# The last 16 tokens of a spectral convolution: one matrix per lag in place of a fourth 8-token block

## The chip, the cores and the metric

The kernel runs on one core of a Trainium2 chip. The metric is the device time of one execution in microseconds (us), the median over the runs shown. The core has a matrix engine (TensorE, PE in the profile; its weight loads are listed apart as PEld), a vector engine (VectorE, DVE), an activation engine (ScalarE, ACT), GpSimd (POOL), and a queue that here issues nearly all transfers (SyncE, SP).

## The reference, cut to what matters

The whole is a four-layer network on 16 images of 128 channels and 28 x 28 = 784 positions: an L1-distance convolution, two quantized convolutions, an additive-attention block with a mixture of experts, and a linear-attention block with a spectral filter (STU). All is fp32. The change touches only the last, the spectral filter on the 784 tokens of each image:

```python
U_plus  = irfft(rfft(phi) * rfft(u))[:sl]            # causal convolution of u with 16 filters
U_minus = irfft(rfft(phi) * rfft(u * sgn))[:sl] * sgn    # the same with alternating signs
out = einsum('btkd,k,kde->bte', U_plus, sigma ** 0.25, M_phi_plus)
    + einsum('btkd,k,kde->bte', U_minus, sigma ** 0.25, M_phi_minus)
    + sum_i shift(u, i) @ M_u[i]                     # three shifts
```

It is computed for the first 784, 392, 196 and 98 tokens with four sets of matrices, and mixed with weights that depend on parameters only. So output token t is a sum over lags l of u[t - l] times a 128 x 128 matrix that depends on the lag alone.

## The kernel before, in words

**Layout of the work.** Images go in pairs. Eight "pairs" of the L1 convolution come one after the other; each is a list of *steps* (264 steps in the first two pairs, 208 in the other six). In a step four filters get their absolute-difference tiles `d` from VectorE (max, L1139 and L1141) or ScalarE (abs, L1137), and TensorE sums each over channels with a selector of 32 columns (L1126): four such products run in four strips of the array. The tiles `d` come from a ring of 10 buffers.

**Other layers beside it.** Everything else is written as generators that yield either `EV` (other engines next) or `PE` (TensorE next). They are run in lanes: `convs` (group norm and quantized convolutions), `chain` (the token lane: `head`, `attend`, `experts`, `linear_attention`, `normed`), and `conv_out` (the spectral filter, `spectral(b)`). The attention scores (`scores`, ScalarE tanh at L727 with TensorE sums at L710) run as `units`, two in a step. In each step a lane gets `rate` turns, rounded over time, so with `RATE_Y` = 0.85 the spectral lane takes 0.85 turns a step. What comes in which order on each engine is thus the order in which the program emits it; TensorE's order is fixed to it. A lane that has nothing ready lets its turn pass. `normed(b)` waits until `spectral(b - 1)` is through.

After the last pair there are no more distances. In this *tail* (`stage["alone"]`) the remaining scores, the token lane and the spectral lane go on, with `RATE_Z` = 0.75 spectral turns a step; scores are then made by VectorE adds and one large tanh (L720, L722).

**The spectral filter of one image.** `normed` leaves the normalized tokens by channel in `ut` (two zero columns ahead) and, transposed by 128, the even and the odd tokens in `up` (two parities, four blocks of up to 128 tokens: 128 + 128 + 128 + 8 = 392). `spectral(b)` makes the even outputs (`to` = 0) and then the odd ones (`to` = 1), 392 columns each, in the accumulator `acc`: three products with `mats_ar` (the shifts of the reference, L1004), and 32 *jobs*. A job has one filter and one parity of the filter's taps: a banded matrix `band` [128, 392] is fetched, four products with the four blocks of `up` as weights (of 392, 264, 136 and 8 columns, L1019) give the filtered tokens `u`; ScalarE copies them to `us` (L1029), and in the next turn a product with the job's mixing matrix `mat` adds them to `acc` (L1022). So there are 64 jobs per image and 1024 in all. `fetch(n)` asks for band and mat two jobs ahead, on SP, into three buffers each.

The matrices are made once: `token_constants` builds the 32 bands, `spectral_weights` the 32 mixing matrices `mats` in DRAM (`mats[k]` with the even taps' filter k, `mats[16 + k]` with the odd). Both belong to the token lane's first work, during pair 0. `sc`, the score matrix, is their scratch before the first scores.

Of the kernel before, what the change touches and what calls it, by code (L numbers as in the profile page):

```python
# [16 lines left out]
T = HW * HW  # L17
# [48 lines left out]
TW = NT * P  # L66
HB = 98

WIN = T // 2 + 2
SPAN = T // 2 + TB  # L70
TH = T // 2
# [6 lines left out]
RING, ROWS = 10, 14  # L78


RATE_X, RATE_Y, RATE_S, RATE_C, RATE_A, RATE_0, RATE_T, RATE_Z = 1.2, 0.85, 2.0, 1.0, 1.5, 0.7, 2.0, 0.75


EV, PE = "other engines", "TensorE"
# [86 lines left out]
def kernel(ctx: ExitStack, tc: tile.TileContext, a: dict, out: bass.AP):  # L171
# [282 lines left out]


    band = [scratch.tile([P, TH], F32, name=f"band{i}") for i in range(2 * NK)]
    mats = [scratch.tile([P, P], F32, name=f"mat{i}") for i in range(2 * NK)]
    mats_ar = [scratch.tile([P, P], F32, name=f"mat_ar{j}") for j in range(NAR)]

    eb_rows = scratch.tile([P, NT, P], F32, name="eb_rows")  # L460
# [58 lines left out]
    def spectral_weights():  # L519


        yield EV
        lw = two.tile([P, NS], F32, tag="lw", name="lw")
        nc.sync.dma_start(lw, rows_of(a["L3_ffn_log_weights"], P))
        gu = two.tile([P, NS], F32, tag="gu", name="gu")
        nc.sync.dma_start(gu, rows_of(a["L3_ffn_gumbel"], P))
        sg = const.tile([P, NK], F32, name="sg")
        nc.sync.dma_start(sg, rows_of(a["L3_ffn_sigma"], P))
        quarter = const.tile([P, NK], F32, name="quarter")
        nc.vector.memset(quarter, 0.25)  # L530
        nc.gpsimd.tensor_tensor(sg, sg, quarter, ALU.pow)
        yield EV
        nc.vector.tensor_tensor(lw, lw, gu, ALU.add)
        s1 = two.tile([P, 1], F32, tag="s1", name="s1")
        nc.vector.tensor_reduce(s1, lw, AX.X, ALU.max)
        nc.vector.tensor_scalar(lw, lw, s1, None, ALU.subtract)
        nc.scalar.activation(lw, lw, AF.Exp)
        yield EV
        nc.vector.tensor_reduce(s1, lw, AX.X, ALU.add)
        nc.vector.reciprocal(s1, s1)  # L540
        soft = const.tile([P, NS], F32, name="soft")
        nc.vector.tensor_scalar(soft, lw, s1, None, ALU.mult)
        hard = const.tile([P, NS], F32, name="hard")
        nc.vector.tensor_reduce(s1, soft, AX.X, ALU.max)
        nc.vector.tensor_scalar(hard, soft, s1, None, ALU.is_equal)
        nc.vector.tensor_tensor(hard, hard, falling[:, :NS], ALU.mult)
        nc.vector.tensor_reduce(s1, hard, AX.X, ALU.max)
        nc.vector.tensor_scalar(hard, hard, s1, None, ALU.is_equal)
        w = const.tile([P, NS], F32, name="mix")
        nc.vector.tensor_tensor(w, hard, soft, ALU.subtract)  # L550
        nc.vector.tensor_tensor(w, w, soft, ALU.add)

        nc.vector.tensor_scalar(mask, ones[:, :1].to_broadcast([P, TH]), hard[:, 0:1], None, ALU.mult)
        for i in range(1, NS):
            nc.vector.tensor_scalar(mask[:, : TH >> i], mask[:, : TH >> i], hard[:, i : i + 1], None, ALU.add)
        yield EV

        def mixed(dst, src):
            nc.vector.tensor_scalar(dst, src[:, 0], w[:, 0:1], None, ALU.mult)
            for i in range(1, NS):  # L560
                nc.vector.scalar_tensor_tensor(dst, src[:, i], w[:, i : i + 1], dst, ALU.mult, ALU.add)

        sources = [a["L3_ffn_M_u"][:, j] for j in range(NAR)]
        sources += [a["L3_ffn_M_phi_" + name][:, k] for k in range(NK) for name in ("plus", "minus")]
        loaded = []

        def fetch():
            if sources:
                t = spare(NS * P).rearrange("p (s e) -> p s e", s=NS)
                nc.sync.dma_start(t, sources.pop(0).rearrange("s d e -> d s e"))  # L570
                loaded.append(t)

        for _ in range(3):
            fetch()
        yield EV
        for j in range(NAR):
            yield EV
            m = three.tile([P, P], F32, tag="mat", name=f"m_ar{j}")
            mixed(m, loaded.pop(0))
            fetch()  # L580
            nc.sync.dma_start(mats_ar[j], m)
        for k in range(NK):
            yield EV
            me = three.tile([P, P], F32, tag="mat", name=f"m_even{k}")
            mo = three.tile([P, P], F32, tag="mat", name=f"m_odd{k}")
            plus = loaded.pop(0)
            mixed(me, plus)
            mixed(mo, loaded.pop(0))
            dif = plus[:, 0]
            nc.vector.tensor_tensor(dif, me, mo, ALU.subtract)  # L590
            nc.vector.tensor_tensor(me, me, mo, ALU.add)
            nc.vector.tensor_scalar(me, me, sg[:, k : k + 1], None, ALU.mult)
            nc.vector.tensor_scalar(mo, dif, sg[:, k : k + 1], None, ALU.mult)
            fetch()
            fetch()
            nc.sync.dma_start(mats[k], me)
            nc.sync.dma_start(mats[NK + k], mo)
        nc.gpsimd.memset(sc, 1.0)
        yield EV

# [351 lines left out]
    def normed(b):  # L952

        yield EV
        t = state.pop(b)[0]
        n4 = one.tile([P, NT, P], F32, tag="ln", name=f"n4_{b}")
        yield from layer_norm(n4, t, 1e-5, f"s{b}")
        while b and b - 1 not in spectral_out:
            yield EV
        yield from to_channels(lambda lo, n: in_rows(ut[:, 2 + lo : 2 + lo + n]), n4, f"n4{b}")  # L960
        tt = one.tile([P, T], F32, tag="tt", name=f"tt{b}")
        yield from to_channels(lambda lo, n: in_rows(tt[:, lo : lo + n]), t, f"t3{b}")
        up = one.tile([P, 2, 4, P], F32, tag="up", name=f"up{b}")
        for par in range(2):
            yield PE
            q = ps(f"up{b}")
            for i in range(4):
                s = 2 + par + 2 * P * i
                nc.tensor.transpose(blk(q, i), ut[:, s : s + 2 * P - 1 : 2], ident)
            yield EV  # L970
            nc.scalar.copy(up[:, par], q.rearrange("p (n c) -> p n c", c=P))
        spectral_in[b] = tt, up

    def spectral(b):
# [19 lines left out]
        for to in range(2):  # L994
            acc = psout.tile([P, 512], F32, tag="acc", name=f"out{b}_{to}")
            for j in range(NAR):
                m = two.tile([P, P], F32, tag="mar", name=f"mar{b}_{to}_{j}")
                nc.sync.dma_start(m, mats_ar[j])
                mar[j] = m
                if j == 0:  # L1000
                    yield EV
                yield PE
                s = 2 + to - j
                nc.tensor.matmul(acc[:, :TH], m, ut[:, s : s + 2 * TH - 1 : 2], start=j == 0, stop=False)  # L1004
            mine = range(32 * to, 32 * to + 32)
            if to == 0:
                fetch(0)
                fetch(1)
            copied = []
            for n in [*mine, None]:  # L1010
                yield PE
                if n is not None:
                    _, k, odd = jobs[n]
                    fetch(n + 2)
                    t, m = got.pop(n)
                    q = small(f"u{b}_{n}")
                    for i in range(4):
                        w = TH - P * i
                        nc.tensor.matmul(q[:, P * i : TH], up[:, to ^ odd, i, :], t[:, :w], start=i == 0, stop=i == 3)  # L1019
                while len(copied) > (stage["alone"] and n is not None):  # L1020
                    u, m0, lag = copied.pop(0)
                    nc.tensor.matmul(acc[:, lag:TH], m0, u[:, : TH - lag], start=False, stop=n is None and not copied)  # L1022
                if n is not None:
                    yield EV
                    if stage["alone"]:
                        u = rows_pool.tile([P, WIN], F32, tag="row", name=f"us{b}_{n}")
                    else:
                        u = two.tile([P, TH], F32, tag="u", name=f"us{b}_{n}")
                    nc.scalar.copy(u[:, :TH], q[:, :TH])  # L1029
                    copied.append((u, m, odd and (to ^ odd)))  # L1030
            yield EV
            s = tt[:, to : to + 2 * TH - 1 : 2]
            y = two.tile([P, TH], F32, tag="y", name=f"ys{b}_{to}")
            nc.vector.tensor_tensor(y, acc[:, :TH], mask, ALU.mult)
            nc.vector.tensor_tensor(s, s, y, ALU.add)
        nc.sync.dma_start(out[b], tt)
        spectral_out.add(b)

# [176 lines left out]
```

## Time and profile before

| | |
|---|---|
| median of three runs | 12013.93 us (12013.17 to 12015.77) |
| the profiled execution's own time | 12013.72 us |
| its span in the profile | 12012.0 us |
| pair 0 / pair 1 / pairs 2 to 7 end at | 916 / 2155 / 3506, 4876, 6252, 7622, 9003, 10393 us |
| tail | 10393 to 12012 us |
| spectral images that end before the tail | 11 of 16 (the 11th at 10349 us) |

How to read it: "busy" is the time in which an engine executes something; an engine's busy share says nothing on what it waits for. TensorE instructions are pipelined, so the durations shown for them overlap and the distance of their starts says more. A stretch is a part of the span between two times, for which busy time is given by engine. A line such as L1019 is a line of the kernel; "u<-band,up" says that a tile u is made of tiles band and up.

### The profile page before, as it was taken

Reading aid. Unit: us, or ns where it says so; the run is one execution under the profiler, and the core shown is the slowest. Engines: PE = TensorE matmul, PEld = TensorE weight load, DVE = VectorE, ACT = ScalarE, POOL = GpSimd, SP = SyncE. Lnnn points to the kernel's source line nnn. Section 1 sums busy time; section 2 is a strip of 40 time slices with the busy share of each in tenths; the row PEclk is TensorE's granted clock in tenths of the full one; section 3 lists DMA queues with packets and bytes.
Section 4 is the critical chain, followed back from the end, with each engine's and each line's share of the span. In section 5 each row is a group of like instructions: output and inputs, shape, how many; then the busy total and the mean of one; then the engine's idle time right before and its main releaser. Section 6 shows DMA issues by size and latency. Waiting matters only on the chain. (4 is left out here: it accounts for less than half of the span.)

```text
span 12012.0 us, 240466 instructions
## 1 busy us (share of the span) xinstructions
PE 11409.5 (95%) x99948; PEld 5214.0 (43%) x99948; DVE 10731.9 (89%) x15051; ACT 10263.3 (85%) x14568; POOL 186.2 (2%) x144
## 2 busy tenths in 40 slices
PE   8989999999999999999999999999999999999999
PEld 3333333444444444444444444444444444454446
DVE  9898789899999999899999999999999889988882
ACT  8884998979979899797998979889898898988882
POOL 0000000000000000000000000000000000000000
PEclk9999999999999999999999999999999999999999
DMA  0110000010110101001010110101110111011113
GB/s 24 58 32 5 1 1 6 17 34 27 33 32 18 35 28 32 24 28 33 26 38 17 31 33 25 31 26 31 34 31 19 29 31 34 27 54 51 54 54 97
DMA packets 376034, 372.49 MB, mean 31 GB/s; under 512 B 40296, under 2 KB 362144, under 8 KB 374944
## 3 DMA queue, kind: packets, MB, share of 16 engines
q1 hardware_dynamic: 374512, 355.35, 10.4%
q8 instruction: 787, 12.89, 0.4%
q14 instruction: 303, 2.48, 0.1%
q10 hardware_dynamic: 432, 1.77, 0.0%
HBM read 340.19 MB, written 16.78 MB: 30 GB/s over the span
## 5 line engine op out<-in xcount | busy, mean ns | idle before, releaser
L727 ACT ACTIVATE row<-wi 128x394 f32<-128x394 f32 x9904 | 5297.0, 625 | 254.1 <-PE sp L710 251.8
L1126 PE MATMUL acc<-d,sel_m 128*32 128x392 f32 x38656 | 5217.3, 502 | 144.2 <-DVE d L1141 133.3
L1139 DVE TENSOR_SCALAR d<-pad,w 128x1568 f32<-128x1568 f32 x4832 | 4783.5, 1031 | 456.9 <-PE acc L1126 454.3
L1126 PE MATMUL acc<-d,sel_a 128*32 128x392 f32 x18176 | 4502.8, 500 | 71.1 <-ACT d L1137 68.8
L1137 ACT ACTIVATE d<-pad,w 128x1568 f32<-128x1568 f32 x2272 | 3581.7, 1609 | 597.7 <-PE acc L1126 581.0
L1141 DVE SCALAR_TENSOR_TENSOR d<-pad,w,d 128x1568 f32<-128x1568 f32 x2112 | 3863.1, 1846 | 8.7
L1126 PEld LDWEIGHTS acc<-d,sel_m 128*32 128x32 f32 x38656 | 1714.0, 111 | 2121.2 <-issue 1653.9
L710 PE MATMUL sp<-row,vz 128*32 128x394 f32 x19808 | 2086.9, 495 | 1.1 <-ACT row L727 1.1
L1126 PEld LDWEIGHTS acc<-d,sel_a 128*32 128x32 f32 x18176 | 1349.4, 110 | 1111.1 <-issue 857.7
L1019 PE MATMUL u<-band,up 128*128 128x392 f32 (+3 forms) x8192 | 1752.9, 355 | 16.4 <-ACT us L1029 14.0
L1019 PEld LDWEIGHTS u<-band,up 128*128 128x128 f32 x8192 | 1330.0, 190 | 964.6 <-issue 281.2
L710 PEld LDWEIGHTS sp<-row,vz 128*32 128x32 f32 x19808 | 728.1, 110 | 1052.9 <-issue 791.1
L722 ACT ACTIVATE th<-th 128x1576 f32<-128x1576 f32 x660 | 969.8, 1521 | 118.4 <-DVE th L720 109.7
L720 DVE TENSOR_SCALAR th<-wi 128x394 f32<-128x394 f32 x2640 | 923.3, 420 | 12.0 <-PE sp L710 9.2
L1022 PE MATMUL out<-us,mat 128*128 128x392 f32 (+1 forms) x2048 | 923.6, 534 | 0.0
L1029 ACT COPY us<-u 128x392 f32<-128x392 f32 x1024 | 491.4, 480 | 480.6 <-PE u L1019 478.5
L710 PE MATMUL sp<-th,vz 128*32 128x394 f32 x5280 | 514.1, 503 | 47.7 <-ACT th L722 47.5
L884 DVE SCALAR_TENSOR_TENSOR t<-ex,gate,t 128x128 f32<-128x128 f32 x896 | 310.7, 347 | 83.9 <-PE ex L880 75.7
L1022 PEld LDWEIGHTS out<-us,mat 128*128 128x128 f32 x2048 | 311.7, 192 | 21.3 <-issue 8.3
L710 PEld LDWEIGHTS sp<-th,vz 128*32 128x32 f32 x5280 | 136.8, 109 | 340.7 <-issue 168.0
L880 PE MATMUL ex<-ew,xt 128*128 128x512 f32 x448 | 236.0, 609 | 37.1 <-DVE t L884 33.2
L795 PE MATMUL av<-vx,sc 128*128 128x129 f32 x1568 | 202.4, 282 | 37.3 <-DVE sc L784 18.7
(257 smaller groups left out, 4415.9 us busy)
## 6 DMA issues: line engine op xcount, KB each, us to landing
band<-band SPq DMA_DIRECT2D x1024, 196.0 KB, 2.4
mat<-mat SPq DMA_DIRECT2D x1024, 64.0 KB, 2.0
L_conv_w<-q_L_conv_w SPq DMA_DIRECT2D x16, 576.0 KB
ew<-in_L_ffn_expert_w_dram SPq DMA_DIRECT2D x16, 512.0 KB
eb<-eb_rows SPq DMA_DIRECT2D x16, 448.0 KB, 4.2
x<-in_x_dram SPq DMA_DIRECT2D x8, 784.0 KB
band<-band_out SPq DMA_DIRECT2D x32, 196.0 KB, 1.9
xr<-in_x_dram SPq DMA_DIRECT2D x8, 784.0 KB, 4.1
```

Of the source, the lines that this page charges most:

```text
L710: nc.tensor.matmul(sp[32 * j : 32 * j + 32, lo : lo + WIN], vz[:, 32 - m : 64 - m], rows[j], start=False, stop=m == Q - 1, skip_group_chec ...
L720: nc.vector.tensor_scalar(th[:, j, :], wi[:, i + Q * j : i + Q * j + WIN], wi[:, i + Q * j : i + Q * j + 1], None, ALU.add)
L722: nc.scalar.activation(th, th, AF.Tanh)
L727: nc.scalar.activation(rows[j], wi[:, i + Q * j : i + Q * j + WIN], AF.Tanh, bias=wi[:, i + Q * j : i + Q * j + 1])
L884: nc.vector.scalar_tensor_tensor(t[:, i, :], q[:, e * P : (e + 1) * P], gate[:, g : g + 1], t[:, i, :], ALU.mult, ALU.add)
L1019: nc.tensor.matmul(q[:, P * i : TH], up[:, to ^ odd, i, :], t[:, :w], start=i == 0, stop=i == 3)
L1022: nc.tensor.matmul(acc[:, lag:TH], m0, u[:, : TH - lag], start=False, stop=n is None and not copied)
L1029: nc.scalar.copy(u[:, :TH], q[:, :TH])
L1126: nc.tensor.matmul(accs[c][32 * j : 32 * j + 32, :NCK], sel[kind][:, 31 - m : 63 - m], d[:, 14 * c : 14 * c + 14, :], start=False, stop=n ...
L1137: nc.scalar.activation(d, window(pad, k, 0, 2 * HW), AF.Abs, bias=w0[:, k, f : f + 1], scale=-1.0)
L1139: nc.vector.tensor_scalar(d, window(pad, k, 0, 2 * HW), w0[:, k, f : f + 1], None, ALU.max)
L1141: nc.vector.scalar_tensor_tensor(d, window(pad, k, 0, 2 * HW), w0[:, k, f : f + 1], d, ALU.max, ALU.add)
```

## The change

The 16 last tokens of an image (784 - 6 x 128, `LAST`) no longer take part as a fourth block of 8 tokens per parity. `up` keeps three blocks per parity, and a job has three products. What is left out is the contribution of the last 16 input tokens to the last 16 output tokens. It is made anew, by lag: for each of the lags 0 to 15 one matrix [128, 128], which is the sum over all filters of the filter's tap at that lag times its mixing matrix. These 16 matrices are made once, at the end of `spectral_weights`, by products of `lag_w` (the taps, 32 filters x lags) with the mixing matrices, read back flat from DRAM, and stored in DRAM as `lag_mats`.

In `spectral`, the first accumulator gets 16 more columns (392 to 407), in which the first `mats_ar` product starts the sum with 408 columns (the last 16 of them over zeros); six turns follow with the lag matrices in groups of three (the last with one), fetched two groups ahead into the buffers of `band`: lag l multiplies the first 16 - l of the last 16 tokens into columns 392 + l to 407. The first two jobs' `fetch` calls move into these turns. At the end of the even half these 16 columns are added to the last 16 tokens of the result by one more VectorE operation. `RATE_Y` goes from 0.85 to 0.93.

```diff
+LAST = T - 6 * P
...
-RATE_X, RATE_Y, RATE_S, RATE_C, RATE_A, RATE_0, RATE_T, RATE_Z = 1.2, 0.85, 2.0, 1.0, 1.5, 0.7, 2.0, 0.75
+RATE_X, RATE_Y, RATE_S, RATE_C, RATE_A, RATE_0, RATE_T, RATE_Z = 1.2, 0.93, 2.0, 1.0, 1.5, 0.7, 2.0, 0.75
...
-    mats = [scratch.tile([P, P], F32, name=f"mat{i}") for i in range(2 * NK)]
+    mats_all = scratch.tile([2 * NK, P * P], F32, name="mats")
+    mats = [mats_all[i].rearrange("(d e) -> d e", e=P) for i in range(2 * NK)]
+
+    lag_mats = scratch.tile([LAST, P, P], F32, name="lag_mats")
...
             nc.sync.dma_start(mats[k], me)
             nc.sync.dma_start(mats[NK + k], mo)
+
+        phi = a["L3_ffn_phi"]
+        lag_w = const.tile([2 * NK, 32], F32, name="lag_w")
+        nc.gpsimd.memset(lag_w, 0.0)
+        for odd in range(2):
+            nc.sync.dma_start(
+                lag_w[odd * NK : odd * NK + NK, odd : LAST : 2],
+                bass.AP(phi.tensor, odd * NK * phi.shape[1] + HB - 1, [[phi.shape[1], NK], [1, LAST // 2]]))
+        yield EV
+        flat = sc.rearrange("p n c -> p (n c)")
+        rhs = {}
+
+        def fetch_flat(g):
+            if g < 8:
+                rhs[g] = flat[: 2 * NK, 2048 * (g % 2) : 2048 * (g % 2) + 2048]
+                nc.sync.dma_start(rhs[g], mats_all[:, 2048 * g : 2048 * g + 2048])
+
+        fetch_flat(0)
+        fetch_flat(1)
+        for _ in range(4):
+            yield EV
+        for g in range(8):
+            yield PE
+            q = ps(f"lag{g}")
+            for j in range(4):
+                nc.tensor.matmul(q[32 * j : 32 * j + 32, :], lag_w, rhs[g][:, 512 * j : 512 * j + 512],
+                                 start=True, stop=True)
+            yield EV
+            fetch_flat(g + 2)
+            o = flat[:, 4096 + 512 * (g % 4) : 4608 + 512 * (g % 4)]
+            nc.scalar.copy(o, q)
+            for j in range(4):
+                nc.sync.dma_start(lag_mats[:, 16 * g + 4 * j : 16 * g + 4 * j + 4, :],
+                                  o[32 * j : 32 * j + LAST].rearrange("l (d e) -> l d e", e=P))
         nc.gpsimd.memset(sc, 1.0)
...
-        up = one.tile([P, 2, 4, P], F32, tag="up", name=f"up{b}")
+        up = one.tile([P, 2, 3, P], F32, tag="up", name=f"up{b}")
...
-            for i in range(4):
+            for i in range(3):
                 s = 2 + par + 2 * P * i
                 nc.tensor.transpose(blk(q, i), ut[:, s : s + 2 * P - 1 : 2], ident)
             yield EV
-            nc.scalar.copy(up[:, par], q.rearrange("p (n c) -> p n c", c=P))
+            nc.scalar.copy(up[:, par], q[:, : 3 * P].rearrange("p (n c) -> p n c", c=P))
...
-                nc.tensor.matmul(acc[:, :TH], m, ut[:, s : s + 2 * TH - 1 : 2], start=j == 0, stop=False)
+                n = TH + LAST if to == 0 and j == 0 else TH
+                nc.tensor.matmul(acc[:, :n], m, ut[:, s : s + 2 * n - 1 : 2], start=j == 0, stop=False)
             mine = range(32 * to, 32 * to + 32)
             if to == 0:
-                fetch(0)
-                fetch(1)
+
+                lags = {}
+
+                def fetch_lags(l):
+                    if l < LAST:
+                        n = min(3, LAST - l)
+                        lags[l] = three.tile([P, TH], F32, tag="band", name=f"lags{b}_{l}")[:, : n * P].rearrange(
+                            "p (l e) -> p l e", e=P)
+                        nc.sync.dma_start(lags[l], lag_mats[l : l + n].rearrange("l d e -> d l e"))
+
+                fetch_lags(0)
+                fetch_lags(3)
+                for l0 in range(0, LAST, 3):
+                    yield PE
+                    fetch_lags(l0 + 6)
+                    m = lags.pop(l0)
+                    for l in range(l0, min(l0 + 3, LAST)):
+                        s = 2 + T - LAST
+                        nc.tensor.matmul(acc[:, TH + l : TH + LAST], m[:, l - l0, :], ut[:, s : s + LAST - l],
+                                         start=False, stop=False)
+                    if l0 == 9:
+                        fetch(0)
+                    if l0 == 12:
+                        fetch(1)
...
-                    for i in range(4):
+                    for i in range(3):
                         w = TH - P * i
-                        nc.tensor.matmul(q[:, P * i : TH], up[:, to ^ odd, i, :], t[:, :w], start=i == 0, stop=i == 3)
+                        nc.tensor.matmul(q[:, P * i : TH], up[:, to ^ odd, i, :], t[:, :w], start=i == 0, stop=i == 2)
...
             nc.vector.tensor_tensor(s, s, y, ALU.add)
+            if to == 0:
+                s = tt[:, T - LAST : T]
+                nc.vector.scalar_tensor_tensor(s, acc[:, TH : TH + LAST], mask[:, TH - 1 : TH], s, ALU.mult, ALU.add)
```

## The prediction

> **What bounds the kernel now.** I read the page's busy shares first, then the stretches (busy time of each engine between two times), then the timeline inside one job, the groups by shape, and the DMA issues.
>
> ```profile
> PE 11409.5 (95%) x99948; PEld 5214.0 (43%) x99948; DVE 10731.9 (89%) x15051; ACT 10263.3 (85%) x14568; POOL 186.2 (2%) x144
> ...
> DVE d L1139 <- PE acc L1126: 454.3, 375, 5.6
> ```
>
> All three engines are near full, TensorE (PE) most; VectorE (DVE) idles 454 us for TensorE to release a tap buffer. The shares are averages, so I cut the span. The next columns are the stretch, its length, and busy time of PE, weight loads (PEld), DVE, ACT.
>
> ```profile
> 3877.00:3923.00 46.00, 46.00 (x433) 20.47 (x426) 40.26 (x33) 45.61 (x74) 0.00 (x0) 1.00 0.14 36
> 5356.00:5402.00 46.00, 44.25 (x406) 19.82 (x408) 41.41 (x34) 46.00 (x75) 0.00 (x0) 1.00 0.14 36
> 6841.00:6887.00 46.00, 44.74 (x401) 20.25 (x402) 43.03 (x36) 46.00 (x75) 0.00 (x0) 1.00 0.13 36
> ...
> 6904.00:7004.00 100.00, 100.00 (x887) 47.84 (x889) 95.32 (x110) 94.44 (x150) 0.00 (x0) 1.00 0.14 38
> ...
> 5881.00:6010.00 129.00, 111.76 (x1113) 45.54 (x1109) 126.78 (x166) 127.44 (x200) 4.13 (x2) 0.95 0.02 8
> ...
> 10391.00:11680.00 1289.00, 1231.66 (x8719) 612.49 (x8711) 1140.72 (x3597) 1084.86 (x991) 20.93 (x16) 0.99 0.17 49
> 11680.00:12012.00 332.00, 315.06 (x1487) 226.65 (x1483) 81.81 (x263) 71.61 (x147) 4.64 (x4) 0.99 0.35 96
> ```
>
> Four regimes. The first three rows are 40 to 85 us into a spectral image (7 to 14 steps after its first mats_ar product): ScalarE (ACT) is full. Later in an image (fourth row) TensorE is full. Between images (fifth) DVE and ACT are at 98 to 99%, TensorE at 87%. After the last pair (sixth, seventh: the tail) TensorE has 95%, DVE 88% and then 25%. So TensorE time taken from a spectral image pays in the second and fourth regime, not in the first and third.
>
> Next, one job where nothing else runs (last image):
>
> ```profile
> 11940.22 0.64 PEld L1019 LDWEIGHTS u<-band,up 128*128 128x128 f32 x4
> 11940.79 0.30 PEld L1022 LDWEIGHTS out<-us,mat 128*128 128x128 f32 x2
> 11941.23 0.85 PEld L1019 LDWEIGHTS u<-band,up 128*128 128x128 f32 x3
> ...
> L1019 PE MATMUL u<-band,up 128*128 128x8 f32 x2048 | 291.2, 214 | 0.0
> ...
> L1029 ACT COPY us<-u 128x392 f32<-128x392 f32 x1024 | 491.4, 480 | 480.6 <-PE u L1019 478.5
> ```
>
> A matmul is two records here (1024 jobs, 2048 records of each width). Jobs start 2.217 us apart. Starts within a job advance by 0.329 twice (392 columns), 0.222 twice (264), 0.115 twice (136). At 8 columns a record's stream is nothing, but its 128-column weight load is not: the first L1022 load starts at 11940.79, 0.11 after the previous one, the next 0.11 later, and the second L1022 product waits until 11941.23. Counted back by one 0.329 stream, the first L1022 product effectively starts at 11940.898; without the 8s it would start 0.115 after the last 136-column record (11940.558), at 11940.673. **The fourth block costs 0.225 us a job**, two weight loads of 0.112.
>
> **What the Trainium skill says.** "TensorE: Matmul & The Clock Gate", section "LDWEIGHTS (loading the stationary operand)": load time goes with the columns of the weights, about 107 ns for 128, whatever the contraction. The trace agrees (0.110 to 0.116 between such loads; the record's 190 ns is longer). "Perfetto Trace Analysis", section "Identifying the Most-Contended Engine": matmul busy share is a poor measure of distance to the limit; hence I use starts, not the 214 ns of the 8-column row. "TensorE: Matmul & The Clock Gate", section "Why this matters for your kernels": outputs at different groups of 32 PSUM partitions run concurrently; the tap sums agree, four starting some 6 ns apart every 0.33 us. "DMA: Bandwidth & Descriptors", section "Latency and other measured facts": about 2 us fixed cost; the median landings of mat and band, 2.0 and 2.4 us, agree.
>
> **The change part by part.** *Removed:* 64 jobs x 0.225 = 14.4 us of TensorE per image, 230 in all; two of eight transposes per image (0.118 each, 0.2); a quarter of the up copy on ACT (586 ns for 512 columns, some 0.12 us less, 32 times, 4 us in all: nothing beside the rest).
>
> *Added per image:* 16 lag products, two records each, bound by weight loads as the nearest row is (lg, L822, 8 columns: starts 0.111 to 0.112 apart): 32 x 0.112 = 3.6 us. They come in six turns. A turn of full-array matmuls among the four-strip tap sums pays for switching: around 7010.6 us the entry takes 0.42 instead of 0.33, its first record 0.43 instead of 0.33, the exit 0.42: 0.3 us x 6 = 1.8 us (0.6 in the tail, where full-array work is usually next). Sixteen more columns in one product: 0.03. One DVE operation of 16 columns (0.15 to 0.2 by the 128x1 and 128x56 rows): 3 us in all; the next image half's first product waits for it, taken as nothing, 0 to +3. Net TensorE per image: -14.4 - 0.2 + 3.6 + 1.8 = **-9.2 us, -147 over 16**.
>
> *Moved, turns of the lane.* An image takes 75 turns before, 81 after (six lag turns). At RATE_Y 0.85 and 0.93 that is 88 and 87 steps, so the supply of later stages does not move. But TensorE work of a step with jobs stays put: 0.85 x (2.217 + 0.3) = 2.14 before, 0.93 x (1.992 + 0.3) = 2.13 after. The saving does not sit in these steps; there are fewer of them (64/0.85 = 75, 64/0.93 = 69), and 6.5 steps with lag products instead. These fall just where the first three rows show ACT full. What helps there is the missing us copy: 0.85 x 0.48 = 0.41 us a step, 2.6 us an image. One step fewer with spectral work (6.7 to about 6.1 us): 0.6. So **3.2 us of 9.2; 11 images end before the tail: -35 us**. Bounds: 0 (ACT stays full) and -101 (all of it).
>
> *Tail:* 5 images, 14.4 + 0.2 - 3.6 - 0.6 = 10.4 each, 52 us. TensorE is the limit, DVE at 88% takes part of it back: I take 80%, -42; bounds -20 and -52. RATE_Z stays 0.75 a step, so an image takes 108 steps instead of 100, and the token lane's normed(12), which waits for spectral_out(11), comes 8 steps later: the heads and scores behind it start later. Steps without scores are short and the work is done later, so 0, up to +16 steps of 3.9 us, two heads late, +62.
>
> *Fetches:* per image six DMAs of up to 196 KB in 512-byte pieces through the band buffers, on SP. Nothing shows such a size in such pieces; nearest are band (2.4 us) and mat (2.0 us), so 2 to 4 us. They are asked for two turns ahead, 2 x 7 us beside the taps, so hidden. fetch(0) and fetch(1) now wait behind lag groups, hidden by two turns or more there. In the last image turns take 1 us and the bands come late once: +5 (0 to +10).
>
> *Setup in pair 0:* eight turns of four 512-column products. The four strips should run together: 2 x 0.43 (start spacing of ex, 512 columns) + 0.3 = 1.2 us, 9 in all; one after another 30. Eight ACT copies of 0.59, 4.7. Its 42 DMAs at 0.32 us issue take 13 us of SP, beside a token lane that has nothing due until pair 1's levels (mats end at 706 us, head(0)'s wi is at 1144). In that stretch TensorE is at 92%: +8, bounds 0 and +30.
>
> Sum: -35 - 42 + 5 + 8 = **-64 us**. The profiled execution took 12013.72 us for a span of 12012.0; 12013.7 - 64 = 11950. The median of the runs, 12013.93, is the same to 0.2 us.
>
> **Rivals.** *B, TensorE binds everywhere:* the 95% and its release waits speak for it, the rows with ACT full against it. Full 147 less setup and fetch, 13: 11880. *C, the gain stays hidden:* ACT and DVE hold the pairs, and late heads in the tail take half: -21 + 13 = -8, 12006. For: 98 to 99% of DVE and ACT between images; against: TensorE at 100% in the fourth row. *D, slower, lag fetches late:* TensorE takes instructions in order, so a lag product waiting for its matrix holds that step's tap sums, and behind them the release of tap buffers to DVE and ACT. 96 groups x 2.4 us = 230: 12014 - 64 + 230 = 12180. It decides from 64/96 = 0.67 us a group. Against it: two turns of cover, and band fetches at the same distance, which TensorE hardly waits for. *E, not what it says:* were the load of mat, not the 8-column block, the limit before L1022, removing the block would save only 0.03 a job, 30 us, less than the 86 us of lag turns and 13 of setup: 12080. The starts above exclude it nearly.
>
> **Numbers.** A (forecast, 11915 to 11985) 0.50, B 0.17, C 0.22, D 0.07, E 0.04. Within 0.2% (24 us, what a measurement of this kernel can tell from no change) lies most of C, 0.16; faster is A, B and the rest of C, 0.73; slower is D and E, 0.11. The range reaches from B's end to C: 11875 to 12010.
>
> **What would show it.** Right: L1019 with three widths; L1022's first product 0.11 us after the last 136-column record; jobs 1.99 us apart in the last image; steps with lag products a little shorter and ACT-full; pairs 5 to 7 us shorter each; a tail of some 1585 us; lag records 0.11 apart. Wrong: TensorE waits on a lag fetch, heads in the tail later than scores, or lag products slower than 0.112 a record.

## The result, and the profile after

After the change the median of four runs is **11938.65 us** (11936.35 to 11939.38), against 12014.41 for four runs of the kernel before beside it: ratio 0.9936, 95% interval 0.9921 to 0.9951, 75.8 us less. The profiled execution has a span of 11937.4 us, 74.6 less than before. Forecast were 11950 and a gain of 64.

| | before | after | difference | forecast |
|---|---|---|---|---|
| pairs 0 and 1 (setup among them) | 2156.1 us | 2157.1 us | +1.0 | +8 |
| pairs 2 to 7 | 8237.0 | 8170.8 | -66.2 | -35 |
| tail (after the last pair) | 1618.9 | 1609.5 | -9.4 | -37 (-42, and +5 of fetches) |

So the sum was met by three terms that missed: the pairs gained nearly twice what was forecast, the tail a quarter. Most of the experiments below look for the reason of the third row.

From the page after, the shares and, of the list of waits, VectorE's and ScalarE's for tap buffers:

```profile
PE 11327.5 (95%) x98444; PEld 5069.4 (42%) x98444; DVE 10741.9 (90%) x15107; ACT 10251.1 (86%) x14546; POOL 178.7 (1%) x145
...
ACT d L1202 <- PE acc L1191: 496.7, 237, 12.6
DVE d L1204 <- PE acc L1191: 433.0, 346, 6.0
```

TensorE is busy 82 us less and keeps its 95%, since the span fell with it. VectorE's wait was 454.3, ScalarE's 581.0. Now the stretches from 20 to 66 us into a spectral image, in three of the pairs. That is where the lag turns stand after the change; the prediction's first three rows lie 20 us later in their images. First before (columns as in the prediction):

```profile
3857.00:3903.00 46.00, 46.00 (x431) 20.07 (x423) 45.86 (x48) 45.61 (x75) 3.02 (x1) 0.97 0.12 30
5336.00:5382.00 46.00, 43.73 (x396) 19.30 (x391) 42.81 (x41) 46.00 (x77) 1.27 (x1) 1.00 0.13 35
6822.00:6868.00 46.00, 44.40 (x403) 20.22 (x402) 45.93 (x41) 46.00 (x77) 0.00 (x0) 1.00 0.13 35
```

And after, with a stretch later in an image, and the tail up to its last image and in it:

```profile
3880.00:3926.00 46.00, 42.33 (x410) 18.45 (x413) 45.85 (x45) 46.00 (x76) 3.61 (x1) 0.96 0.11 29
5342.00:5388.00 46.00, 44.45 (x425) 18.55 (x421) 43.35 (x38) 46.00 (x74) 0.00 (x0) 1.00 0.11 30
6816.00:6862.00 46.00, 44.98 (x415) 21.00 (x413) 46.00 (x44) 46.00 (x72) 0.00 (x0) 1.00 0.11 29
...
6904.00:7004.00 100.00, 100.00 (x887) 46.22 (x886) 94.25 (x110) 91.61 (x145) 0.00 (x0) 1.00 0.15 41
...
10328.00:11617.00 1289.00, 1214.56 (x8511) 583.10 (x8504) 1169.66 (x3710) 1095.58 (x997) 21.18 (x16) 0.99 0.18 50
11617.00:11938.00 321.00, 302.78 (x1295) 210.32 (x1293) 67.59 (x223) 73.93 (x153) 4.63 (x4) 0.98 0.40 109
```

The regimes are the same: ScalarE full early in an image, TensorE full later. One row stands out: the first 1289 us of the tail hold *more* VectorE work than before (1169.66 against 1140.72 us), though the change adds only one short operation per image there. 17 of these 29 us belong to the scores (VectorE's work on `th` in the same stretches is 935.48 us against 918.88). Work has come into the tail.

One job of the last image, from the timeline of weight loads, and from the groups by shape the narrowest tap block and the largest lag product:

```profile
11811.82 1.62 PEld L1081 LDWEIGHTS u<-band,up 128*128 128x128 f32 x6
11813.37 0.31 PEld L1084 LDWEIGHTS out<-us,mat 128*128 128x128 f32 x2
11813.82 1.62 PEld L1081 LDWEIGHTS u<-band,up 128*128 128x128 f32 x6
...
L1081 PE MATMUL u<-band,up 128*128 128x136 f32 x2048 | 405.6, 280 | 0.0
L1065 PE MATMUL out<-ut,lags 128*128 128x16 f32 x32 | 6.2, 270 | 0.0
```

Six loads and two a job where there were eight and two; the blocks have 392, 264 and 136 columns; jobs follow 1.993 us apart (2.217 before; forecast 1.99). The lag product's 270 ns is, like the 214 ns of the old 8-column row, not a cost: six records of a turn start within 0.579 us, 0.116 apart (forecast 0.112).

### The profile page after: what moved, and what is told of

It reads as the page before. It is cut to its first block, busy times and chain, and to the rows that moved or that the text cites. A ratio compares the mean times of both kernels' runs of the same rounds, so it can differ in the third digit from the quotient of the medians.

```text
span 11937.4 us, 237767 instructions
## 1 busy us (share of the span) xinstructions
PE 11327.5 (95%) x98444; PEld 5069.4 (42%) x98444; DVE 10741.9 (90%) x15107; ACT 10251.1 (86%) x14546; POOL 178.7 (1%) x145
## 4 chain that ended last, share of the span: by engine, by line
PE 48%; DVE 17%; ACT 14%; issue 2%; POOL 0%; DMA 0%; ACTq 0%; DVEq 0%; SPq 0%; POOLq 0%
PE acc L1191 17%; PE u L1081 10%; PE sp L749 9%; ACT row L766 8%; DVE d L1206 7%; DVE d L1204 6%; PE out L1084 4%; ACT d L1202 4%; PE conv_ps L397 2%; PE ex L919 1%; DVE th L759 1%; ACT th L761 1%; PE av L834 1%; PE acc L1177 1%; DVE mx L810 0%
## 5 line engine op out<-in xcount | busy, mean ns | idle before, releaser
L749 PE MATMUL sp<-row,vz 128*32 128x394 f32 x19728 | 2120.9, 495 | 1.1 <-ACT row L766 1.1
L1081 PE MATMUL u<-band,up 128*128 128x392 f32 (+2 forms) x6144 | 1633.7, 402 | 27.0 <-ACT us L1091 21.8
L1081 PEld LDWEIGHTS u<-band,up 128*128 128x128 f32 x6144 | 1096.7, 190 | 973.9 <-issue 270.8
L1084 PE MATMUL out<-us,mat 128*128 128x392 f32 (+1 forms) x2048 | 843.3, 494 | 0.0
```

The costliest lines, as they stand in the source:

```text
L749: nc.tensor.matmul(sp[32 * j : 32 * j + 32, lo : lo + WIN], vz[:, 32 - m : 64 - m], rows[j], start=False, stop=m == Q - 1, skip_group_chec ...
```

## The experiments

Twelve kernels, in the order of the questions. In the table, "units" counts the score units that fall into the tail (one large tanh each), and "third head" is the step, counted from the start, at which the token lane starts its third image; both are read from the trace. A median stands beside its own runs of the kernel before, so the ratio is what compares kernels. The times of the pairs and of the tail are from one profile each; pairs 0 and 1, the same instructions in before and in the five kernels made from it, take 2150.7 to 2156.1 us in these profiles, so a difference of 5 us there says nothing.

| kernel | median us | ratio to before (95%) | pairs 2 to 7 | tail | units | third head |
|---|---|---|---|---|---|---|
| before | 12014 | 1 | 8237.0 | 1618.9 | 660 | 566 |
| after | 11938.65 | 0.9936 (0.9921 to 0.9951) | 8170.8 | 1609.5 | 670 | 572 |
| e3_no_fourth | 11877.6 | 0.9887 (0.9872 to 0.9902) | 8165.8 | 1560.1 | 660 | 566 |
| e6_twice | 12186.44 | 1.0143 (1.0128 to 1.0158) | 8348.5 | 1682.5 | 660 | 566 |
| e1_rate85 | 12010.04 | 0.9997 (0.9989 to 1.0006) | 8107.2 | 1745.3 | 730 | 573 |
| e2_rate93 | 12059.66 | 1.0038 (1.0023 to 1.0053) | 8298.4 | 1607.7 | 652 | 565 |
| e4_pair2_rate | 11939.42 | 0.9939 (0.9923 to 0.9956) | 8171.9 | 1609.7 | 672 | 573 |
| e5_ratez81 | 11949.79 | 0.9946 (0.9931 to 0.9960) | 8172.6 | 1616.2 | 670 | 572 |
| e10_empty_turns | 11999.57 | 0.9988 (0.9981 to 0.9994) | 8118.7 | 1728.6 | 730 | 573 |
| e12_no_fourth93 | 11901.8 | 0.9906 (0.9889 to 0.9923) | 8199.6 | 1550.1 | 652 | 565 |
| e8_release | 11901.68 | 0.9906 (0.9891 to 0.9921) | 8165.2 | 1579.4 | 652 | 563 |
| e9_in_jobs | 11905.26 | 0.9910 (0.9893 to 0.9926) | 8172.1 | 1574.8 | 660 | 566 |
| e11_jobs_release | 11880.47 | 0.9888 (0.9874 to 0.9903) | 8160.0 | 1567.8 | 652 | 563 |
| e13_release_all | 11911.47 | 0.9915 (0.9900 to 0.9930) | 8163.2 | 1588.1 | 656 | 562 |

**What is the fourth block worth, alone?** Two kernels made from before: one leaves it out and puts nothing in its place, one issues its product a second time.

```diff
 # e3_no_fourth
-                    for i in range(4):
+                    for i in range(3):
-                        nc.tensor.matmul(q[:, P * i : TH], up[:, to ^ odd, i, :], t[:, :w], start=i == 0, stop=i == 3)
+                        nc.tensor.matmul(q[:, P * i : TH], up[:, to ^ odd, i, :], t[:, :w], start=i == 0, stop=i == 2)
 # e6_twice
-                        nc.tensor.matmul(q[:, P * i : TH], up[:, to ^ odd, i, :], t[:, :w], start=i == 0, stop=i == 3)
+                        nc.tensor.matmul(q[:, P * i : TH], up[:, to ^ odd, i, :], t[:, :w], start=i == 0, stop=False)
+                    nc.tensor.matmul(q[:, 3 * P : TH], up[:, to ^ odd, 3, :], t[:, : TH - 3 * P], start=False, stop=True)
```

> The kernel before without the fourth product of each job (8 columns), and nothing in its place: the contribution of the last 16 input tokens to the last 16 output tokens is left out. RATE_Y 0.85, 75 turns as before. It takes 1024 x 0.225 = 230 us off TensorE. Theory A (TensorE binds only part of the time; share of the lane's matmuls on the chain is 73% beside the pairs and 96% in the tail, and other engines take some over): 100 to 160 us gain, so 11855 to 11915 us, of it 50 to 60 us in the tail. Rival B (TensorE binds everywhere): 215 to 230 us gain, 11785 to 11800. Rival C (hidden in the pairs): only the tail's 70 us, 11945.

> The kernel before with the fourth product of each job issued twice, RATE_Y 0.85; the last 16 input tokens' contribution is thereby counted twice. It adds what leaving the block out takes away: 1024 x 0.225 = 230 us of TensorE. Theory A (TensorE binds more of the time when it has more to do): more than the 136 us that leaving it out gave, 160 to 225 us more than before, 12175 to 12240; jobs 2.44 us apart in the last image. Rival B (the price of two weight loads is only partly real): jobs under 2.35 us apart, under 120 us more.

In the last image of e6_twice (timeline of matmuls) the second 8-column product has a line of its own, L1020:

```profile
12110.74 1.62 PE L1019 MATMUL u<-band,up 128*128 128x392 f32 x8
12112.21 0.37 PE L1020 MATMUL u<-band,up 128*128 128x8 f32 x2
12112.43 0.90 PE L1023 MATMUL out<-us,mat 128*128 128x392 f32 x2
12113.18 1.62 PE L1019 MATMUL u<-band,up 128*128 128x392 f32 x8
```

Jobs are 2.44 us apart (12110.74 to 12113.18): +0.22 for one product more, as -0.224 for one less. The price of 0.225 us a job holds in both directions, 230 us over 1024 jobs. Of these 230, leaving it out gives 136 (59%), doubling it costs 172 (75%). By place, e3 gains 71 us in pairs 2 to 7 of the 158 that 11 images x 64 jobs x 0.225 amount to (45%), and 59 of 72 in the tail (82%, forecast 80%).

**Is RATE_Y needed?** One kernel is after with the old rate, one is before with the new.

```diff
 # e1_rate85, from after; e2_rate93, from before, is the reverse
-RATE_X, RATE_Y, RATE_S, RATE_C, RATE_A, RATE_0, RATE_T, RATE_Z = 1.2, 0.93, 2.0, 1.0, 1.5, 0.7, 2.0, 0.75
+RATE_X, RATE_Y, RATE_S, RATE_C, RATE_A, RATE_0, RATE_T, RATE_Z = 1.2, 0.85, 2.0, 1.0, 1.5, 0.7, 2.0, 0.75
```

> The changed kernel with RATE_Y back at 0.85; nothing else differs. Theory A (TensorE's saving pays only where a step is bound by TensorE, and the rate decides in which steps the saving lies): at 0.85 the saving lies in the steps with jobs themselves (0.85 x 0.225 = 0.19 us of TensorE a step), and the first spectral image blocks the quantized convolutions less, so the third head starts some 6 steps earlier and 10 score units stay in the pairs (660 th activations in the tail, as before the change, where the change has 670). Against it, an image takes 95 steps instead of 87, so normed waits a few steps longer. Expected 11925 to 11955 us, the change itself being 11939. Rival B (the higher rate is what made room for the lag turns): heads come 8 steps later from image to image, over 700 th activations in the tail, 11960 to 12000 us.

> The kernel before with RATE_Y 0.93 alone. Theory A: no TensorE work goes, so no gain; the convolutions beside the first spectral image end some 6 steps later, as in the change, so the tail gets some 10 score units more: 12010 to 12035 us, th activations about 670. Rival B (a good part of the 76 us comes from the rate): 11960 to 11990 us.

My first theory, that after at 0.85 would keep most of the gain, fell: 12010, all of it gone. The pairs are *shorter* by 130 us than before, but 81 turns at 0.85 take 95 steps, `normed` waits for the image before it, the heads behind it come late and 730 score units are left for a tail that grew by 126 us. The rate alone, on the other hand, costs before 46 us (0.38%): 61 more in pairs 2 to 7, 11 less in the tail. From its first step to its last, each of the 11 images before the tail takes fewer steps: 987 of 6.761 us in all instead of 1086 of 6.656, which is 555 us less, but 99 more steps outside an image take some 610. That was more than expected, and the units did not rise to 670, as I had thought, but fell to 652.

Two more kernels split this. e10_empty_turns is e3 (no fourth block, old rate) with six PE turns per image that issue nothing; e12_no_fourth93 is e3 at the new rate.

```diff
 # e10_empty_turns, from e3_no_fourth
             if to == 0:
+                for _ in range(6):
+                    yield PE
                 fetch(0)
 # e12_no_fourth93, from e3_no_fourth
-RATE_X, RATE_Y, RATE_S, RATE_C, RATE_A, RATE_0, RATE_T, RATE_Z = 1.2, 0.85, 2.0, 1.0, 1.5, 0.7, 2.0, 0.75
+RATE_X, RATE_Y, RATE_S, RATE_C, RATE_A, RATE_0, RATE_T, RATE_Z = 1.2, 0.93, 2.0, 1.0, 1.5, 0.7, 2.0, 0.75
```

> The kernel before without the fourth product (as in the run that left it out, 11878 us), RATE_Y 0.85, plus six turns of the spectral lane per image in which nothing is issued, at the place of the lag turns; the contribution of the last 16 input tokens to the last 16 output tokens is left out. Theory A (turns, not work: at 0.85 the spectral lane needs 95 steps for 81 turns, so normed, the next head and the scores come later, and score units that fitted into the pairs are left to the tail): about 730 th activations in the tail against 660, pairs shorter and tail longer, 11940 to 11975 us. Rival B (the lag products' own TensorE work costs the 132 us that lie between the change at 0.85 and the run without the fourth product): 11875 to 11885 us, 660 th activations.

> The kernel before without the fourth product and with RATE_Y 0.93, 75 turns; the contribution of the last 16 input tokens to the last 16 output tokens is left out. It asks why 0.93 alone costs 46 us with the fourth product in. Theory A (the rate moves the lane's TensorE work into fewer steps; with the product in, 0.93 x (2.217 + 0.3) = 2.34 us a step exceeds what a step bears, without it 2.13 us is what the steps had before): no cost to speak of against 0.85, 11870 to 11895 us, pairs 8000 to 8030 us longer than pair 1's end as at 0.85 (8166), within 10. Rival B (a higher rate costs whatever the job): 46 us more than at 0.85, 11915 to 11930.

The large tanh of the tail's scores, from the page of e3_no_fourth and then of e10_empty_turns (the count x is the number of units):

```profile
L722 ACT ACTIVATE th<-th 128x1576 f32<-128x1576 f32 x660 | 970.4, 1524 | 104.1 <-DVE th L720 96.6
```

```profile
L722 ACT ACTIVATE th<-th 128x1576 f32<-128x1576 f32 x730 | 1072.0, 1520 | 131.3 <-DVE th L720 117.9
```

**Six empty turns cost 122 us** (11877.6 to 11999.6; 11940 to 11975 were expected), without one instruction: the pairs shrink by 47 us, and the tail, with 70 units more, grows by 168. The heads fall behind from image to image: the third is 7 steps late, the thirteenth 34 (1692 against 1658). The turns act through the rate and through what they hold (the next question); at 0.85 no run parts the two. And the rate alone costs 24 us where the fourth block is gone (e12), half of the 46 with it: neither "nothing", as one theory had it, nor as much as before. So 0.93 isn't a gain of the change but what it pays for its six turns.

**Why is the third head late at 0.93 too, and the tail short of its gain?** In after the third head starts at step 572, six later than before, the scores some five steps later throughout, and 10 units more are left. Here the rate had been my suspect; the next kernel keeps the old rate up to pair 2. Beside it one gives the spectral lane of the tail back its pace, for the theory that 108 steps an image instead of 100 hold up heads there.

```diff
 # e4_pair2_rate, in ahead() of after
+        if not stage["alone"]:
+            conv_out.rate = 0.85 if stage["pair"] < 3 else RATE_Y
 # e5_ratez81, from after: RATE_Z
-RATE_X, RATE_Y, RATE_S, RATE_C, RATE_A, RATE_0, RATE_T, RATE_Z = 1.2, 0.93, 2.0, 1.0, 1.5, 0.7, 2.0, 0.75
+RATE_X, RATE_Y, RATE_S, RATE_C, RATE_A, RATE_0, RATE_T, RATE_Z = 1.2, 0.93, 2.0, 1.0, 1.5, 0.7, 2.0, 0.81
```

> The changed kernel with the spectral lane's rate 0.85 up to the third pair (pair 2, where the first spectral image runs beside the convolutions of pair 1) and 0.93 from there on. Theory A (at 0.93 the spectral lane holds the bank that it shares with the convolutions more often, the levels of pair 1 come 6 steps later, and with them the third head and all later scores, so 10 score units move into the tail): the third head starts at step 566 as before the change instead of 572, th activations in the tail 660, tail 15 to 25 us shorter, pairs 5 to 15 us longer, 11925 to 11939 us. Rival B (the units moved for another reason): th activations stay at 670 and the time at 11939.

> The changed kernel with RATE_Z 0.81 instead of 0.75, so that an image of 81 turns takes 100 steps in the tail, as it did before the change. The prediction's step on the tail (late heads cost 0 to 62 us there): if late heads cost, scores 14 and 15 start earlier and the tail is 10 to 40 us shorter, 11900 to 11930 us. Rival (the tail is bound by TensorE's sum, whatever the order): tail within 8 us, 11931 to 11947 us.

Both theories fell. With the old rate the head is no earlier (573, 672 units, 11939.42). A faster spectral lane makes the tail 7 us longer (11 in the medians) instead of shorter: its last two heads start some 40 us earlier, but the tile `wi` that their scores need is made 13 and 27 us later. So earlier heads inside the tail gain nothing; the units that come *into* it cost.

What holds the head was then read from pair 1's quantized convolutions, which run beside the first spectral image. The tile y of those convolutions between 2206 and 2460 us (durations as lowest, median, highest ns; first and last start), of before, then of after:

```profile
L400 ACT ACTIVATE y<-conv_ps,bias,inv x7: 656/660/686, 2223.6 to 2395.1; 128x392 f32<-128x392 f32 x7
```

```profile
L402 ACT ACTIVATE y<-conv_ps,bias,inv x7: 659/696/713, 2224.7 to 2428.3; 128x392 f32<-128x392 f32 x7
```

The last one is 33 us, some five steps, later. The lanes `convs` and `conv_out` are each other's `other`: a lane gets no PE turn while the other one `holds`, that is between a PE turn of the other and its next EV turn. The six lag turns follow each other, and the `mats_ar` turns before them, with no EV turn between; so the convolutions stand still. A kernel that lets go before each lag turn tests it:

```diff
 # e8_release, from after
                 for l0 in range(0, LAST, 3):
+                    yield EV
                     yield PE
```

> The changed kernel with one more yield to the other engines ahead of each lag turn; work, rate and number of PE turns are the same. A lane that has just done a TensorE turn keeps the shared bank from the other lane until its next turn of the other kind; the lag turns follow one another without such a turn, so the quantized convolutions of pair 1 stand still for six steps. Theory A: with it the third head starts at step 566 instead of 572, 660 th activations in the tail instead of 670; tail 15 to 25 us shorter, pairs 5 to 15 longer, 11922 to 11935 us. Rival B (the six steps come from elsewhere): 572, 670, 11939 us.

The same tile in e8_release:

```profile
L402 ACT ACTIVATE y<-conv_ps,bias,inv x7: 657/676/723, 2222.1 to 2380.5; 128x392 f32<-128x392 f32 x7
```

The last convolution is 48 us earlier, the third head at 563, and the tanh rows of after and of e8_release count the difference:

```profile
L761 ACT ACTIVATE th<-th 128x1576 f32<-128x1576 f32 x670 | 983.0, 1525 | 113.4 <-DVE th L759 100.0
```

```profile
L761 ACT ACTIVATE th<-th 128x1576 f32<-128x1576 f32 x652 | 955.8, 1522 | 110.1 <-DVE th L759 97.9
```

18 units less in the tail, 30.1 us off it (1.7 us a unit), 6 off the pairs, **37 us in all from a line that computes nothing**. That is more than expected; before at 0.93 (e2) has the third head at 565 and 652 units as well, so without the hold the change gets what its rate gives. This one is shown: the line adds no instruction, TensorE has 98444 records in both, and only the order in which the lanes get their turns differs. With the order the form of 18 units changes: beside the pairs a unit is four short tanh on ScalarE, in the tail VectorE adds and one large tanh.

**What do the lag products cost where they need no turns?** In e9_in_jobs two lags at a time ride in the first eight jobs' turns, in buffers of their own, at the old rate; e11_jobs_release lets go before every `mats_ar` product too, and e13_release_all does that to e8_release.

```diff
 # e9_in_jobs, from after: RATE_Y 0.85, the loop of lag turns removed, fetch(0) and fetch(1) back
 # behind mats_ar, lags[l] a tile two.tile([P, 2 * P], F32, tag="lags")
                     t, m = got.pop(n)
+                    if n < 8:
+                        ml = lags.pop(2 * n)
+                        for l in (2 * n, 2 * n + 1):
+                            s = 2 + T - LAST
+                            nc.tensor.matmul(acc[:, TH + l : TH + LAST], ml[:, l - 2 * n, :], ut[:, s : s + LAST - l],
+                                             start=False, stop=False)
+                        fetch_lags(2 * n + 4)
 # e11_jobs_release, from e9_in_jobs; e13_release_all, the same edit from e8_release
                 mar[j] = m
-                if j == 0:
-                    yield EV
+                yield EV
                 yield PE
```

> The changed kernel with RATE_Y 0.85 and no lag turns: two lag matrices at a time, in buffers of their own, are used at the start of the first eight jobs' turns, so an image takes 75 turns as before. Theory A (what the change lost against leaving the block out, 61 us, is mostly turns and rate): 16 images x 32 records x 0.112 = 57 us of TensorE more than without the fourth product, and no further switches; half of it shows beside the pairs, most in the tail: 11900 to 11925 us, 660 th activations. Rival B (the lag products themselves cost what the change lost): 11935 to 11945 us.

> The version with lag products inside the first eight jobs' turns and RATE_Y 0.85, plus a yield to the other engines ahead of each of the three products with mats_ar, not of the first alone, so that these turns too release the shared bank. Theory A (holding the bank delays the convolutions and with them heads and scores): two turns less of standstill, third head at step 563 or 564 instead of 566, 4 to 8 score units fewer in the tail, 11890 to 11902 us against 11905. Rival (no further effect): 11903 to 11908.

> The changed kernel with a yield to the other engines ahead of each lag turn (11902 us) and ahead of each mats_ar product as well. Theory A: some 2 steps more for the convolutions beside the first image, 646 to 650 th activations, 11890 to 11900 us. Rival: no effect, 11899 to 11904.

e9_in_jobs is 28 us above e3_no_fourth: that is the price of the lag work itself (with its setup), against the 136 that it stands for. After is 33 above e9: the six turns, with what they do to the rate and to the hold; e9 also has buffers of its own for the lags, which no run tries alone. e11_jobs_release, at 11880.47, is the fastest that makes the whole sum: 134 us below before and 58 below after, its interval clear of after's, and 10 below the range that was expected. Its stretch of the tail up to the last image shows VectorE with 1147.88 us of work where after has 1169.66:

```profile
10312.00:11600.00 1288.00, 1226.95 (x8461) 600.51 (x8462) 1147.88 (x3609) 1084.74 (x1009) 19.43 (x15) 0.99 0.19 54
```

The release of `mats_ar` is not a part of the change and might help before as well; that was not run. e13_release_all missed: the third head is one step earlier again (562), yet it is 10 us slower than e8_release, with 656 units and 9 us more tail. By the trace its fourth head comes at step 647 and not at 641, and 4 units more, at 1.7 us, would be 7 of the 9 us. Why the same edit gains 25 us in e9 and loses 10 in e8 stays open.

## Why the prediction was right, and where it was right by chance

**The price of a job: right.** 0.225 us forecast, 0.224 (leaving out) and 0.22 (doubling) measured. The method was to count starts, and not the 214 ns of the row. The Trainium skill's "TensorE: Matmul & The Clock Gate", section "LDWEIGHTS (loading the stationary operand)", makes the load time go with the columns of the weights, whatever the contraction; by its formula 128 columns take an estimated 107 ns. Lag records 0.116 apart, which have 1 to 16 columns to stream, agree within a tenth. The 0.224 refutes rival E, which needed 0.03.

**Lag turns: nearly right.** A turn among four-strip work takes 0.424 to enter, 0.579 for six records and 0.184 from there to the next tap product, 0.86 us over the 0.33 that passes between tap products anyway; forecast 0.97. The exit had been taken as 0.42, from wider products, whose own stream of 0.33 is in it.

**Beside pairs, -35: its main term right, two terms put at nothing.** A step is counted here from its first tap product to that of the next. The lag turns stand in steps 3 to 9 of an image, counted from its first `mats_ar` product; the prediction had read steps 7 to 14. On average these seven steps fell from 6.835 to 6.186 us, 0.65 each, where 0.41 was forecast. But around each change of pairs seven steps in a row are slow, some 9.1 us each (the 35 steps at the five changes from pair 2 on: 317.0 us before, 317.9 after). Before, the seven at the last change are just these steps of the tenth image; after, most of them lie ahead of its lag turns. In the other ten images the step falls from 6.575 to 6.204 us: **0.37 each, 2.6 us an image, as forecast**. The reason fits too: ScalarE is busy for 6.55 of the 6.575 us before and for all of the 6.204 after, so what helps is that a lag turn needs no `us` copy. In e9, where the lag products ride in turns that do have the copy, the same steps do not fall (6.673).

The step that failed is "TensorE work of a step with jobs stays put", and with it that nothing else moves. Behind the tenth step of an image, with the slow steps set aside, a step falls from 6.584 to 6.564 us: 0.02 each, but 939 of them make 19 us. The first three steps of the ten images fell from 6.406 to 5.960, 13 us in all, and why stays open. These two are the 31 us that the forecast lacks; the 19 is a small difference of large sums in two profiles. "One step fewer" per image held roughly (1077 steps in 11 images, 1086 before). Ten units fewer are made beside the pairs as well, and no run shows what that alone is worth there. That the pairs gain so much from the edit itself is seen in e9: with units and third head as before it gains 64.9 there.

**Tail, -42: right for the edit, wrong for the kernel.** With the lags inside the jobs the tail fell by 44 (e9). In after it fell by 9.4. The step that failed is "the supply of later stages does not move": turns per image were counted, 88 against 87 steps, and the difference was right (the trace has 99 and 98, since a lane also lets turns pass, as while the other holds); not counted was whom these turns keep waiting. At 1.2 to 1.7 us a unit (e12 against e3, 8 units and 10.0 us; e8 against after) the 10 units that came into the tail are an estimated 12 to 17 of the 33 missing us. What the rest is, no run isolates: e9, which has no lag turns in its tail, is still 5 us shorter there than e8 with 8 units fewer.

**Late heads in the tail, 0 to +62: taken as nothing, rightly.** Counted from the start of the tail, the 15th head is 21 us later than before and the 16th no later; e5, which has both some 40 us earlier, gained nothing.

**Fetches, +5: 1.4.** TensorE waited twice for a lag matrix or what it delayed, both in the last image (timeline of its start; the wait in brackets):

```profile
11793.56 3.15 PE L1065 MATMUL out<-ut,lags 128*128 128x7 f32 x14 [0.69 <-DMA lags<-lag_mats]
11797.38 3.01 PE L1081 MATMUL u<-band,up 128*128 128x392 f32 x6 [0.68 <-DMA band<-band]
```

Rival D needed 0.67 us in each of 96 groups; it had it in one. The extra VectorE operation (0.232 us) held the next half's `mats_ar` products for 3.1 us over all images, at the upper end of the 0 to 3 allowed.

**Setup, +8: +1.** The row of its products shows that four strips run together, 64 records in 8.5 us:

```profile
L628 PE MATMUL lag<-sc,lag_w 32*32 32x512 f32 x64 | 8.5, 600 | 0.0
```

The rest lay beside other work: pairs 0 and 1 together grew by 1.0 in these two profiles, and by 2.9 between the averages of the six profiles without the setup and of the eight with it.

**The rivals.** B (TensorE binds everywhere, 11880) isn't true in the pairs, where e3 realises 45%, and empty turns cost without any TensorE work; but -66 lies nearly as near to B's -101 there as to the forecast's -35. C (hidden, 12006) is refuted by the 66 us of the pairs. C's second half, late work in the tail, is the part that came true, by another cause than the one named. So the total came out by luck: the pairs gave 31 us more than forecast and the tail, with its fetches, 28 less. That a rate of 0.93 costs 24 to 46 us by itself stood in none of them.

## What to carry to other kernels

A tiny fp32 product costs its weight loads, and pricing it by the distance of starts gives the size of the edit within a few per cent. How much of it is realised depends on which engine fills the steps where the edit will stand; read those very steps, and set aside first what is slow there for another reason: seven slow steps after a change of pairs would make 0.37 us a step look like 0.65. Where lanes hand each other turns, ask of every turn added what it holds and for whom: six turns with no instruction in them cost 122 us here, one release gained 37. If work can ride in turns that exist, it needs neither extra turns nor the rate that pays for them.

## What was not expected of the hardware

Coming back from full-array products to four-strip work costs nearly the same here whether the product is wide or narrow. From the start of the last record to the next tap product pass 0.184 us behind a lag product and 0.422 behind a 392-column one (medians). Without the 0.116 and 0.329 that lie between such records anyway, 0.07 and 0.09 remain. And one product more and one less are not worth the same: 172 us lost and 136 gained for the same 0.22 us a job. That the next limit is closer on one side than on the other would explain it; no run shows which.
